# Graph attention with a conditioned self feature on one core: some loads moved in SP's queue, three setup matmul groups split into 32-output pieces

## The chip, the core and the metric

The kernel runs on one core of a Trainium2 chip. A core has a matrix engine (TensorE, PE in the profile, with PEld for its weight loads), three engines for elementwise work (VectorE, DVE; ScalarE, ACT; GpSimd, POOL), a queue engine that here issues nearly all transfers (SyncE, SP), and 16 DMA engines that carry them out. SBUF is the on-chip memory of 128 partitions, PSUM holds what TensorE writes, HBM (DRAM) is outside. The metric is device time in microseconds. All data are float32, but for the integer mask.

## The reference

For each of 16 batches there are 512 rows of 512 features (`x`), one condition vector of 512 (`q`), and an integer adjacency `adj` of 512 x 512 x 11 labels, of which only what concerns the first 20 rows is used.

```
row_zero  = x.sum(-1) == 0
self_feat = [x, where(row_zero, 0, q)] @ W_self.T + b_self
for d in 0, 1:
    A    = (adj, adj transposed)[d][:, :, :20, :]
    kv   = self_feat[:, :20]
    qh   = (self_feat @ Wq[d].T + bq[d])      in 16 heads of 32
    kh   = (kv        @ Wk[d].T + bk[d])      in 16 heads of 32
    aff  = where(A.sum(-1) > 0, qh . kh / sqrt(32), -9e15) + A @ w_bias + b_bias
    w    = softmax(aff over the 20)
    out += (w @ kv) @ Wout[d] per head + bout[d]
result = x + relu(self_feat + out)
```

## The kernel before, in words

**Setup.** Much is folded into small tables before the loop. `kv_terms` (L531) makes the 320 columns of `kv` for all batches (20 rows x 16 batches) in four PSUM banks `ps_kv`, the reduction cut in four steps k that follow the arrival of their weights. ACT turns them into `kvT`. `key_rows` (L577) multiplies `kvT` by the key weights into `ps_k` for each direction d and each of four groups of 128 features; ACT and DVE turn the result into `khD`, the keys as differences from the first one. `keys` (L660) folds the query weights into the keys: it is called in 22 bursts of 8 matmuls (the last of 4) of shape 32 x 128 into `ps_g`, which ACT (L684) and DVE (L686) scale into stages `st`; the stages go to SBUF for batch 0 and to DRAM (`g_d`, `g1_d`) for the others. Between the bursts, other setup work is put by a written list (`plan`, L714): `values` (L636, `ps_v`, the rows of `kv` times the output weights, parked in DRAM), `bias_scores`, the flags of the first batches (`ps_nz`), and the self feature of batch 0 (`self_feat`, L191, `ps_sf`).

**Forms of a matmul.** A program matmul of float32 shows as two weight loads and two matmul records. A 128-output matmul writes 128 PSUM partitions and uses the whole array; in the 32-output form the same work is four matmuls, each with 32 of the 128 weight columns, which write 32 partitions each and stand in four quarters of the array. The loop's scores and products and `ps_sf` have the 32-output form already; `ps_kv`, `ps_k` and `ps_v` have the 128-output one (`ps_v` of the last 64 rows a 64-output one).

**Loop.** 16 batches b, each in four tiles nt of 128 rows. The order on every engine is written out by hand and kept as written. A tile's step on TensorE is `scores` (L346: 64 matmuls into `ps_s`, from the self feature and the folded keys `g`). `weigh` (L364), `expo`, `normal` and `turn` make the softmax on DVE, ACT, POOL and DVE: the mask and bias tile `full` is added, the maximum taken and subtracted, the exponential taken, and after the next tile's start the sum, the division and the transpose. `full` is built by POOL (`full_add`, L336) from `cq` (the scores' biases) and `both` (the masks, spread by ACT). Each tile also carries parts for the next batch: its self feature by seven block products (`product`, L246, into `ps_a`, `ps_d`, `ps_c`; `x_sum` on POOL makes their differences; `partial` and `joined` on DVE combine them, `partial` with the row flags `nz`), its masks (`mask_mul`, `mask_count`, `mask_sum`, `mask_spread`), and its row sums (`row_sum` on ACT from `xn`, from which `row_mask` writes the flags to `nz_d`). In tile 2 TensorE makes the output of the batch before (`attend`, L417, 24 matmuls into `ps_o`: the output run); `finish` adds the self feature on DVE (four times) and takes the relu on ACT (four times), and POOL adds x (`residual`).

**Queues.** SP issues the loop's transfers in the order of the code and stops at each until what it waits for is done. `behind` (L95) puts a load behind an instruction kept in `done`. An iteration has 22 transfers there: flags `nz` (L173), biases `cq` in four (L116), masks `adj` in two halves (h = 0: "first masks", of tiles 0 and 1; h = 1: "second masks"), raw rows `xn` in two, x in two, keys `g` in two halves (L124), values `vd` in four, outputs in four, the write of `nz_d`. In the compiled program each transfer also waits until the one eight places earlier has landed.

Of the kernel before, what the change touches and what calls it, by code (L numbers as in the profile page):

```python
# [13 lines left out]
P = 128  # L14
# [4 lines left out]
def gat_kernel(  # L19
# [20 lines left out]
    nc = tc.nc  # L40
# [70 lines left out]
    def load_adj(b, h, ins=None):  # L111
        t = adjs[b, h] = load.tile([P, 2, S * L], I32, tag="adj", name=f"adj{b}_{h}", bufs=3)
        a = adj[b, h * 2 * P : (h + 1) * 2 * P].rearrange("(t p) d m l -> p t (d m l)", p=P)
        behind(nc.sync.dma_start(t, a), ins)

    def load_cq(b):  # L116
        cqs[b] = load.tile([P, HL, S], F32, tag="cq", name=f"cq{b}")
        for a in range(HL):
            nc.sync.dma_start(
                cqs[b][bass.ts(a, R)].rearrange("p h m -> p (h m)"),  # L120
                cq_d[b : b + 1, bass.ts(a, HL)].rearrange("b h d m -> b (h d m)").partition_broadcast(R),
            )
# [50 lines left out]
    def load_nz(b, ins=None):  # L173
        nzs[b] = load.tile([P, N], F32, tag="nz", name=f"nz{b}")
        behind(nc.sync.dma_start(nzs[b], nz_d[b : b + 1].partition_broadcast(P)), ins)
# [117 lines left out]

    def joined(b, n, key, f, l):

        nc.vector.tensor_add(
            block(b, f, l), parts[b, key][:, : 2 * HN].rearrange("p (i n) -> p i n", i=2), us.pop((b, n))
        )

# [132 lines left out]
    def finish(b, o, banks):  # L432

        for c in range(C):
            add = nc.vector.tensor_add(o[:, c], banks[c], sfs[b][:, c])  # L435
            if c == 0:
                done["add"] = add
        for c in range(C):
            relu = nc.scalar.activation(o[:, c], o[:, c], AF.Relu, bias=bo[:, c : c + 1])  # L439
            if c == 0:  # L440
                done["relu"] = relu

    def residual(b, c, o):
# [9 lines left out]
    with tc.tile_pool(name="setup", bufs=1) as sp, tc.tile_pool(name="ps_acc", bufs=4, space=PSUM) as acc["pool"]:  # L453
# [18 lines left out]
        with tc.tile_pool(name="setup_k", bufs=1) as sk:  # L472
# [56 lines left out]
            kv_ps = [bank(f"ps_kv{fc}") for fc in range(C)]  # L529

            def kv_terms(fc, k):  # L531
                nc.tensor.matmul(  # L532
                    kv_ps[fc][:, :BM], ws_v[:, k, bass.ts(fc, P)], xkv[:, k],
                    start=(k == 0), stop=(k == C - 1),
                )

            for k in range(2):
                for fc in range(C):
# [38 lines left out]
            def key_rows(d, jc):  # L577

                ps = bank(f"ps_k{d}{jc}")
                for k in range(C):  # L580
                    nc.tensor.matmul(  # L581
                        ps[:, :BM], wk_sb[d][:, k, bass.ts(jc, P)], kvT[:, k],
                        start=(k == 0), stop=(k == C - 1),
                    )
                p3 = ps[:, :BM].rearrange("p (b m) -> p b m", m=NG)
                kh0 = msk.tile([P, B], F32, tag="kh0", name=f"kh0{d}{jc}", bufs=4)
                nc.scalar.activation(kh0, p3[:, :, 0], AF.Identity, bias=bk_sb[:, d, jc : jc + 1])
                nc.vector.scalar_tensor_tensor(
                    khD[:, d * C + jc].rearrange("p (b m) -> p b m", m=ND), p3[:, :, 1:],
                    bk_sb[:, d, jc : jc + 1], kh0.unsqueeze(2).to_broadcast([P, B, ND]),  # L590
                    ALU.add, ALU.subtract,
                )
# [18 lines left out]
        with tc.tile_pool(name="setup_g", bufs=4) as sg:  # L611
# [24 lines left out]
            def values(t, ds, k):  # L636


                rows = min(P, BM - t * P)
                if k == 0:  # L640
                    held[1 + t // 2] = bank(f"ps_v{t}{ds[0]}")
                ps = held[1 + t // 2]
                for i, d in enumerate(ds):
                    nc.tensor.matmul(  # L644
                        ps[bass.ds(i * rows, rows)], kvT[:, k, bass.ds(t * P, rows)], wo_sb[:, d, k],
                        start=(k == 0), stop=(k == C - 1),
                    )
                if k == C - 1:
                    v = msk.tile([P, H * S], F32, tag="full", name=f"v{t}{ds[0]}")[:, :F]
                    nc.vector.tensor_copy(v, ps)  # L650
                    for i, d in enumerate(ds):
                        nc.gpsimd.dma_start(
                            vw_d[d, :, bass.ds(t * P, rows)].rearrange("c r w -> r c w"),
                            v[bass.ds(i * rows, rows)].rearrange("p (c w) -> p c w", c=C),
                        )
# [113 lines left out]
    with tc.manual_schedule():  # L769
# [11 lines left out]
        for b in range(B):  # L781
# [7 lines left out]
            for nt in range(NT):  # L789
# [64 lines left out]
                if nt == 1:  # L854
                    if b > 0:
                        joined(b, 2, "c", 0, 1)
                    if b > 0 and more:
                        load_nz(b + 1, done["exp"])
                        load_cq(b + 1)
                    normal(*prev)  # L860
                    if b > 0 and more:
                        load_adj(b + 1, 1, done["normal"])
                    if b == 0:
                        self_feat(0, 1, 1)
                    for g in range(2):
                        scores(b, nt, g, ps[g])
                    if b == 0:
                        self_copy(0, 1, 1)
                    if last:
                        for c in (0, 1):  # L870
                            nc.scalar.activation(biased[:, c], sfs[b][:, c], AF.Identity, bias=bo[:, c : c + 1])
                    s = weigh(b, nt, pair)
                    expo(s)
                    turn(*prev)
                    if more:
                        x_sum(b + 1, 2)
                        x_sum(b + 1, 3)
                    full_add(b, 2)
                    if last:
                        for c in (0, 1):  # L880
                            nc.gpsimd.tensor_add(biased[:, c], biased[:, c], xs[b][:, c])  # L881

                if nt == 2:
                    if more:
                        mask_mul(b + 1, 0)
                    else:
                        full_add(b, NT - 1)
                    if b > 0:
                        banks = [bank(f"ps_o{b - 1}_{q}", q) for q in range(4)]
                        attend(b - 1, banks)  # L890
                        o = work.tile([P, C, N], F32, tag="o", name=f"o{b - 1}")
                        finish(b - 1, o, banks)
                        if b + 2 < B:
                            load_xn(b + 2, 0, done["add"])
                            load_xn(b + 2, 1, done["relu"])
                    normal(*prev)
                    for g in range(2):
                        scores(b, nt, g, ps[g])
                    if more:
                        product(b + 1, 1)  # L900
                        product(b + 1, 2)
                    s = weigh(b, nt, pair, (lambda: partial(b + 1, 1, 0, 0)) if more else None)
                    expo(s)
                    turn(*prev)
                    if b > 0 and more:
                        load_keys(b + 1, range(2), done["exp"])
                    if more:
                        full_add(b, NT - 1)
                    if b > 0:
                        for c in (0, 1):  # L910
                            residual(b - 1, c, o)

                if nt == 3 and more:
                    mask_count(b + 1, 0)
                    product(b + 1, 6)
                    new_self(b + 1)
                    joined(b + 1, 1, "d", 0, 0)
                    x_sum(b + 1, 4)
                    if b + 2 < B:
                        for j in range(4):  # L920
                            row_sum(b + 2, j)
                    normal(*prev)
                    partial(b + 1, 2, 0, 1)
                    mask_sum(b + 1, 0)
                    if b > 0:
                        load_keys(b + 1, range(2, C), done["masks"])
                    mask_spread(b + 1, 0)
                    for g in range(2):
                        scores(b, nt, g, ps[g])
                    product(b + 1, 7)  # L930
                    product(b + 1, 5)
                    s = weigh(b, nt, pair, lambda: partial(b + 1, 3, 1, 1))
                    expo(s)
                    turn(*prev)
                    if b > 0:
                        residual(b - 1, 2, o)
                        store()
                        load_values(b)
                        residual(b - 1, 3, o)
                    full_add(b + 1, 0)  # L940
# [105 lines left out]
```

## Time and profile before

| what | us |
|---|---|
| median of 3 runs (591.52 to 592.68) | 591.74 |
| the profiled execution, whole | 593.27 |
| its span, first to last instruction | 591.5 |
| TensorE busy | 578.7 (98%) |
| VectorE busy | 492.3 (83%) |
| ScalarE, GpSimd busy | 395.6, 384.2 |
| setup, up to the first scores | 92.5 |

The span is the time from the first to the last instruction; the whole execution has 1.77 us around it. In the chain that ended last a row holds the start, the length and the work (engine, tile, line, number of records), "issue" being time in which the engine waited for nothing that the profile shows. In rows of a timeline the first two numbers are the same, and in brackets stands the idle time before. Rows of DMA issues give the count, the size and the median time from issue to landing. DVE's row of digits is its busy share in tenths in 40 equal slices of the span (14.8 us each). "q8 instruction" is the queue that brings TensorE's instructions to the core.

### The profile page before, as it was taken

To read this page: it belongs to the slowest core of one execution; us is meant where nothing else is said; L and a number is where in the kernel's file an instruction comes from. 1 tells how busy PE (TensorE), PEld (TensorE's weight loads), DVE (VectorE), ACT (ScalarE), POOL (GpSimd) and SP (SyncE) were. 2 spreads that over 40 slices of the span, in tenths; PEclk is the share of its full clock that TensorE was granted. 3 is DMA by queue.
4 is the path that set the end of the run, shared out by engine and by line. 5 is a ranking of instruction groups with operands and counts; after the bars stand their busy time and mean duration, and the time that the engine had idled before them with its cause. 6 is when DMAs were issued, how large, how long until landed. Compare 5 with 4: busy or idle time off the path is not lost.

```text
span 591.5 us, 30038 instructions
## 1 busy us (share of the span) xinstructions
PE 578.7 (98%) x13180; PEld 439.7 (74%) x13180; DVE 492.3 (83%) x785; ACT 395.6 (67%) x1162; POOL 384.2 (65%) x351
## 2 busy tenths in 40 slices
PE   8999999999999999999999999999999999999994
PEld 6654547888978687787878787788787878787882
DVE  0495565889898888999999999888989898989896
ACT  1234644587877677768686868677787877777661
POOL 2315663638677675758686777675858677776774
PEclk9999999999999999999999999999999999999997
DMA  8998999857848485767676766757585748582503
GB/s 294 385 406 299 332 376 329 257 126 199 223 154 229 155 236 148 206 168 209 184 208 163 223 173 202 171 181 208 164 217 170 216 149 232 158 238 85 167 13 142
DMA packets 98129, 124.10 MB, mean 210 GB/s; under 512 B 19952, under 2 KB 70160, under 8 KB 95952
## 3 DMA queue, kind: packets, MB, share of 16 engines
q1 hardware_dynamic: 96752, 120.31, 67.1%
q8 instruction: 103, 1.69, 1.2%
q0 software_dynamic: 672, 1.36, 1.0%
q10 hardware_dynamic: 576, 0.53, 0.3%
q14 instruction: 26, 0.21, 0.1%
HBM read 82.30 MB, written 40.24 MB: 207 GB/s over the span
## 4 chain that ended last, share of the span: by engine, by line
PE 94%; DVE 3%; DMA 1%; issue 1%; ACT 0%; POOL 0%; SPq 0%; DVEq 0%; POOLq 0%; ACTq 0%
PE ps_s L353 44%; PE ps_a L279 17%; PE ps_c L279 8%; PE ps_o L426 6%; PE ps_d L279 4%; PE ps_v L644 3%; PE ps_k L581 3%; PE ps_sf L202 2%; DMA ws_q<-in_wsT 1%; PE ps_kv L532 1%; DVE o L435 0%; PE ps_nz L186 0%; DVE wt L415 0%; DVE ps_s L371 0%; DVE sm L406 0%
## 5 line engine op out<-in xcount | busy, mean ns | idle before, releaser
L353 PEld LDWEIGHTS ps_s<-g,sf 128*32 128x32 f32 x8192 | 264.0, 110 | 19.8 <-issue 12.2
L353 PE MATMUL ps_s<-g,sf 128*32 128x152 f32 x8192 | 277.3, 293 | 0.5 <-ACT st L684 0.5
L334 ACT COPY both<-add 32x80 f32<-32x80 f32 x512 | 130.9, 256 | 54.8 <-DVE add L325 49.0
L408 POOL TENSOR_TENSOR s<-s,sm 128x640 f32<-128x640 f32 x63 | 80.3, 1275 | 98.0 <-DVE sm L407 98.0
L341 POOL TENSOR_TENSOR full<-cq,both 128x640 f32<-128x640 f32 x64 | 100.1, 1565 | 30.3 <-issue 24.3
L314 ACT ACTIVATE prod<-adj,wb_sb 128x80 f32<-128x80 int32 x330 | 112.5, 432 | 0.0
L380 ACT ACTIVATE s<-s 128x640 f32<-128x640 f32 x63 | 46.5, 738 | 69.4 <-DVE s L375 69.0
L444 POOL TENSOR_TENSOR o<-o,x 128x512 f32<-128x512 f32 x60 | 75.9, 1285 | 0.0
L367 DVE TENSOR_TENSOR full<-ps_s,full 128x608 f32<-128x608 f32 x63 | 49.1, 779 | 32.1 <-PE ps_s L353 26.6
L406 DVE TENSOR_REDUCE sm<-s 128x32 f32<-128x640 f32 x63 | 50.9, 808 | 8.8 <-ACT s L380 8.6
L279 PE MATMUL ps_a<-t,ws_s 128*32 128x246 f32 x960 | 55.5, 370 | 0.0
L371 DVE TENSOR_REDUCE ps_s<-full 128x32 f32<-128x640 f32 x63 | 52.2, 828 | 2.2
L415 DVE STREAM_TRANSPOSE wt<-s 128x640 f32<-128x640 f32 x63 | 52.8, 839 | 0.1
L375 DVE TENSOR_TENSOR s<-full,ps_s 128x640 f32<-128x640 f32 x63 | 51.6, 818 | 1.1
L426 PE MATMUL ps_o<-wt,vd 32*32 32x512 f32 (+5 forms) x816 | 40.8, 581 | 3.7 <-DVE wt L400 2.0
L279 PEld LDWEIGHTS ps_a<-t,ws_s 128*32 128x32 f32 x960 | 32.2, 110 | 15.5
L325 DVE TENSOR_REDUCE add<-prod 128x80 f32<-128x960 f32 x32 | 36.8, 1150 | 6.3 <-ACT prod L314 4.4
L244 POOL TENSOR_TENSOR t<-x 128x492 f32<-128x492 f32 x30 | 34.4, 1148 | 10.1 <-DVE full L367 5.2
L439 ACT ACTIVATE o<-o,bo 128x512 f32<-128x512 f32 x60 | 38.2, 708 | 0.6 <-POOL biased L881 0.6
L435 DVE TENSOR_TENSOR o<-ps_o,sf 128x512 f32<-128x512 f32 x60 | 36.8, 672 | 1.0 <-PE ps_o L426 1.0
L286 DVE SCALAR_TENSOR_TENSOR u<-nz,qw,ps_a 128x246 f32<-128x246 f32 x90 | 36.6, 449 | 0.0
L244 POOL TENSOR_TENSOR t<-x,t 128x492 f32<-128x492 f32 x30 | 34.4, 1147 | 1.2
(238 smaller groups left out, 722.7 us busy)
## 6 DMA issues: line engine op xcount, KB each, us to landing
g_d<-st SPq DMA_DIRECT2D x16, 1064.0 KB, 5.9
g<-g_d SPq DMA_DIRECT2D x28, 608.0 KB, 5.2
out_T<-o SPq DMA_DIRECT2D x60, 256.0 KB, 4.7
xn<-in_xn SPq DMA_DIRECT2D x28, 512.0 KB, 3.6
x<-in_xT SPq DMA_DIRECT2D x28, 512.0 KB, 4.3
adj<-in_adj SPq DMA_DIRECT2D x32, 440.0 KB, 5.0
nz<-nz_d SPq DMA_DIRECT2D x14, 256.0 KB, 4.0
wk<-in_wkT SPq DMA_DIRECT2D x2, 1024.0 KB, 8.0
```

The lines of the kernel that those rows point to most:

```text
L244: nc.gpsimd.tensor_sub(t, one, two)
L279: nc.tensor.matmul(to, lhs, x[:, k], start=start, stop=stop, skip_group_check=n != 2)
L314: nc.scalar.activation(p[:, :, l], a[:, :, l], AF.Identity, scale=wb_sb[:, l : l + 1])
L334: nc.scalar.copy(adds[b, h][bass.ts(a, R), :, g], add[r].rearrange("p (t m) -> p t m", t=2))
L341: nc.gpsimd.tensor_add(f, cqs[b].unsqueeze(1).to_broadcast(shape), adds[b, nt // 2][:, nt % 2].unsqueeze(2).to_broadcast(shape),)
L353: nc.tensor.matmul(bank[bass.ts(a, R), bass.ts(j, WD // HL)], sfs[b][:, k, bass.ds(nt * P + (2 * g + j) * R, R)], keys[:, k, a], start=(k ...
L371: nc.vector.tensor_reduce(mx, f, AX.X, ALU.max)
L375: nc.vector.tensor_sub(s, f, mx.unsqueeze(3).to_broadcast(full))
L408: done["normal"] = nc.gpsimd.tensor_mul(s, s, sm.unsqueeze(3).to_broadcast(full))
L415: nc.vector.transpose(wts[b][:, nt], s.rearrange("p a h m -> p (a h m)"))
L426: nc.tensor.matmul(banks[a][bass.ds(at // 2 * DH, n * DH)].rearrange("p (t n) -> p t n", n=32), vd[r, bass.ds(at * DH, n * DH)], wt[r, :, ...
L444: nc.gpsimd.tensor_add(o[:, c], o[:, c], xs[b][:, c])
```

## The change

Two independent parts.

In the setup, each matmul of `ps_kv`, `ps_k` and `ps_v` becomes four (two for the last 64 rows of `ps_v`) of 32 outputs. The sums, their order over k and the results are the same.

In the loop, nine transfers of an iteration move in SP's queue. The flags `nz` of the next batch go from tile 1 to tile 2, behind `finish`; they still wait for the latest exponential, which is now that of tile 1 instead of tile 0. The two loads of `xn` wait for the last of the four output additions and for the second relu, instead of the first of each. The second masks go from tile 1, where they waited for `normal`, to the end of tile 2, behind its exponential, and the biases `cq` follow them there. The first half of the keys goes from the end of tile 2 (behind its exponential) into tile 3, behind `joined`; the second half stays behind `mask_sum` in tile 3. In the after, the order in SP's queue is: flags, xn, xn, second masks, four biases, two outputs, two halves of keys, an output, four values, an output, x, x, write of the flags, first masks.

```diff
@@ -293,7 +293,7 @@
 
     def joined(b, n, key, f, l):
 
-        nc.vector.tensor_add(
+        done["joined"] = nc.vector.tensor_add(
             block(b, f, l), parts[b, key][:, : 2 * HN].rearrange("p (i n) -> p i n", i=2), us.pop((b, n))
         )
 
@@ -433,11 +433,10 @@
 
         for c in range(C):
             add = nc.vector.tensor_add(o[:, c], banks[c], sfs[b][:, c])
-            if c == 0:
-                done["add"] = add
+            done["add"] = add
         for c in range(C):
             relu = nc.scalar.activation(o[:, c], o[:, c], AF.Relu, bias=bo[:, c : c + 1])
-            if c == 0:
+            if c == 1:
                 done["relu"] = relu
 
     def residual(b, c, o):
@@ -529,10 +528,11 @@
             kv_ps = [bank(f"ps_kv{fc}") for fc in range(C)]
 
             def kv_terms(fc, k):
-                nc.tensor.matmul(
-                    kv_ps[fc][:, :BM], ws_v[:, k, bass.ts(fc, P)], xkv[:, k],
-                    start=(k == 0), stop=(k == C - 1),
-                )
+                for a in range(HL):
+                    nc.tensor.matmul(
+                        kv_ps[fc][bass.ts(a, R), :BM], ws_v[:, k, bass.ds(fc * P + a * R, R)], xkv[:, k],
+                        start=(k == 0), stop=(k == C - 1),
+                    )
 
             for k in range(2):
                 for fc in range(C):
@@ -578,10 +578,11 @@
 
                 ps = bank(f"ps_k{d}{jc}")
                 for k in range(C):
-                    nc.tensor.matmul(
-                        ps[:, :BM], wk_sb[d][:, k, bass.ts(jc, P)], kvT[:, k],
-                        start=(k == 0), stop=(k == C - 1),
-                    )
+                    for a in range(HL):
+                        nc.tensor.matmul(
+                            ps[bass.ts(a, R), :BM], wk_sb[d][:, k, bass.ds(jc * P + a * R, R)], kvT[:, k],
+                            start=(k == 0), stop=(k == C - 1),
+                        )
                 p3 = ps[:, :BM].rearrange("p (b m) -> p b m", m=NG)
                 kh0 = msk.tile([P, B], F32, tag="kh0", name=f"kh0{d}{jc}", bufs=4)
                 nc.scalar.activation(kh0, p3[:, :, 0], AF.Identity, bias=bk_sb[:, d, jc : jc + 1])
@@ -641,10 +642,11 @@
                     held[1 + t // 2] = bank(f"ps_v{t}{ds[0]}")
                 ps = held[1 + t // 2]
                 for i, d in enumerate(ds):
-                    nc.tensor.matmul(
-                        ps[bass.ds(i * rows, rows)], kvT[:, k, bass.ds(t * P, rows)], wo_sb[:, d, k],
-                        start=(k == 0), stop=(k == C - 1),
-                    )
+                    for a in range(rows // R):
+                        nc.tensor.matmul(
+                            ps[bass.ds(i * rows + a * R, R)], kvT[:, k, bass.ds(t * P + a * R, R)], wo_sb[:, d, k],
+                            start=(k == 0), stop=(k == C - 1),
+                        )
                 if k == C - 1:
                     v = msk.tile([P, H * S], F32, tag="full", name=f"v{t}{ds[0]}")[:, :F]
                     nc.vector.tensor_copy(v, ps)
@@ -854,12 +856,7 @@
                 if nt == 1:
                     if b > 0:
                         joined(b, 2, "c", 0, 1)
-                    if b > 0 and more:
-                        load_nz(b + 1, done["exp"])
-                        load_cq(b + 1)
                     normal(*prev)
-                    if b > 0 and more:
-                        load_adj(b + 1, 1, done["normal"])
                     if b == 0:
                         self_feat(0, 1, 1)
                     for g in range(2):
@@ -890,6 +887,8 @@
                         attend(b - 1, banks)
                         o = work.tile([P, C, N], F32, tag="o", name=f"o{b - 1}")
                         finish(b - 1, o, banks)
+                        if more:
+                            load_nz(b + 1, done["exp"])
                         if b + 2 < B:
                             load_xn(b + 2, 0, done["add"])
                             load_xn(b + 2, 1, done["relu"])
@@ -903,7 +902,8 @@
                     expo(s)
                     turn(*prev)
                     if b > 0 and more:
-                        load_keys(b + 1, range(2), done["exp"])
+                        load_adj(b + 1, 1, done["exp"])
+                        load_cq(b + 1)
                     if more:
                         full_add(b, NT - 1)
                     if b > 0:
@@ -915,6 +915,8 @@
                     product(b + 1, 6)
                     new_self(b + 1)
                     joined(b + 1, 1, "d", 0, 0)
+                    if b > 0:
+                        load_keys(b + 1, range(2), done["joined"])
                     x_sum(b + 1, 4)
                     if b + 2 < B:
                         for j in range(4):
```

## The prediction

> **What bounds the kernel now.** I read the page's shares first, then the chain that ended last, then SP's queue in one iteration.
>
> ```profile
> DVE  0495565889898888999999999888989898989896
> ...
> q8 instruction: 103, 1.69, 1.2%
> ...
> PE 94%; DVE 3%; DMA 1%; issue 1%; ACT 0%; POOL 0%; SPq 0%; DVEq 0%; POOLq 0%; ACTq 0%
> ```
>
> TensorE makes 94% of the chain: time is won only where PE's work shortens or where PE stands. The chain through the setup, and one piece of batch 0:
>
> ```profile
> 11.45 2.39 PE ps_kv L532 x8
> ...
> 17.43 8.94 PE ps_k L581 x32
> ...
> 27.34 2.35 PE ps_k L581 x8
> ...
> 37.86 2.36 PE ps_k L581 x8
> ...
> 41.69 1.91 PE ps_v L644 x4
> ...
> 51.54 1.01 PE ps_v L644 x4
> ...
> 59.41 1.73 PE ps_sf L202 x32
> ...
> 83.97 1.87 PE ps_v L644 x8
> ...
> 110.66 0.77 issue
> ```
>
> ps_sf is already in the 32-output form: 16 matmuls of 256 columns, four sets of four, 1.73 us, or 0.43 us a set, which is 1.69 ns a column (a program matmul is two records, one for each half of the f32 work). The 128-output form in the same place, between two bursts of keys, takes 1.91 for two matmuls of 512 columns, the same 1024 columns.
>
> In the loop the chain is PE without a break but for one place, the output run (attend, L426, 48 records):
>
> ```profile
> 164.12 2.60 PE ps_o L426 x47
> ...
> 195.02 1.04 PE ps_o L426 x25
> 196.45 2.10 PE ps_o L426 x23
> ...
> 226.92 0.98 PE ps_o L426 x4
> ...
> 258.97 2.17 PE ps_o L426 x48
> ...
> 289.44 2.17 PE ps_o L426 x48
> ...
> 381.08 1.05 PE ps_o L426 x27
> ...
> 413.08 2.84 PE ps_o L426 x48
> ...
> 444.22 2.17 PE ps_o L426 x48
> ```
>
> From one uncut run to the next is 30.47 us (258.97 to 289.44). The iteration that begins at 164.12 takes 30.90, at 195.02 31.90, at 226.92 32.05, at 381.08 32.00, at 413.08 31.14: 0.43 + 1.43 + 1.58 + 1.53 + 0.67 = 5.6 us lost in five of fifteen runs. The cut moves: record 25, then 4, then not in the run, later 27. An iteration is 784 records (four tiles of 128, seven products of 32, 48), each a weight load and a matmul, and by the compiled program 10 waits: 1,578 instructions, 42 over a multiple of 256, so a mark every 256 instructions comes 21 records earlier each time. 25 to 4 is that step, and 1.69 MB in 103 transfers is 16.4 KB each. PE stands at the edge of a block of instructions that has not arrived.
>
> **The change, part by part.** *Setup matmuls in 32-output form.* 16 matmuls of ps_kv, 32 of ps_k, 16 of ps_v with 128 outputs and 8 with 64 become 272 of 32 outputs. Priced at 1.69 ns a column, four sets of 320 take 2.16 us and two of 512 1.73.
> - Values: eight stretches of 1.91, so 8 x 0.18 = 1.44; the 64-row ones 2 x 0.14 (1.01 to 0.87) and 0.14 (1.87 to 1.73). Gross 1.9. About 0.4 returns as waiting: in the middle of the setup two bursts of keys wait for DVE copies that stand behind the mask's reductions, which hang on POOL. Net 1.5.
> - Key rows: four stretches of 2.35, 4 x 0.19 = 0.76, and 0.29 in the first one (8.94 against 8.65). DVE's third slice (29.6 to 44.4 us) is at 9 tenths, so its copies set the pace for part of this, and the first stretch waits for ACT's kvT. I take 0.4.
> - ps_kv: 0.23 at 11.45; the later stretch (0.09) is not what kvT waits for. 0.2.
>
> Together -2.1; ends -3.2 (all of it) and 0 (every saving becomes a wait or a drain, below).
>
> *A rule against it.* The Trainium skill (TensorEngine Tiling (Array Packing), Key Properties) says that a change of the array's tiling mode drains TensorE. The after still changes shape at every burst, so by that rule alone this part is worth nothing and the sum would be +0.7 instead of -1.4. The trace shows no such drain on entering ps_sf behind a burst of another shape: 1.69 ns a column is the rate of the loop's scores too (4.00 us for 124 records of 152 columns, last row below: 1.70). What the 128-output form loses, it loses at its entry.
>
> *800 more PE instructions.* 200 more matmuls at four instructions each; 800 = 3 x 256 + 32, so every block edge of the loop falls 16 records earlier. In batch 0 PE stands 0.77 us (110.66) at an edge among the products, whose records of 246 columns last 52 ns by the rate above: it needs the block 16 x 52 = 0.8 us sooner. It asks for it one block earlier, among scores (32 ns a record), 0.5 sooner: +0.3; ends -0.8 (the stall goes) and +0.8 (the block comes no sooner).
>
> *The loop's loads.* SP's queue in the iteration whose output run is at 319.92:
>
> ```profile
> 314.45 0.37 SPq L114 DMA_DIRECT2D adj<-in_adj  x1
> 317.69 0.34 SPq L175 DMA_DIRECT2D nz<-nz_d  x1
> 318.08 2.95 SPq L119 DMA_DIRECT2D cq<-cq_d  x4
> 321.14 0.39 SPq L114 DMA_DIRECT2D adj<-in_adj  x1
> 323.93 4.10 SPq L109 DMA_DIRECT2D xn<-in_xn  x2
> 330.65 0.38 SPq L130 DMA_DIRECT2D g<-g_d  x1
> 331.12 1.50 SPq L449 DMA_DIRECT2D out_T<-o  x2
> 334.95 0.38 SPq L130 DMA_DIRECT2D g<-g_d  x1
> ```
>
> Flags, biases and second masks (317.69 to 321.5) leave the stretch before the output run. Would that free the instruction block? It is asked for about one block earlier: some 102 records of scores of 32 ns, 3.3 us before the run begins (for the cut at record 25). The flags are issued 2.2 us before the run, after the request; what is in flight at the request are the first masks, issued 5.5 us before the run and landing in 5.0 (median, below). They stay. So I count no gain there; ends -5.6 (all stalls go) and +4. By the 21-record step the edges of before lie at records 46, 25 and 4, then at 48, 27 and 6, then at 50 of the run; 16 earlier they cut it at 30, 9, 32, 11 and 34, and in two iterations fall 10 records ahead of it. Behind record 32 the run's second matmul shape begins, before which PE finishes the first anyway; an edge there costs like the one at 46 (0.4): 1.5 + 1.5 + 0.4 + 1.5 + 0.4 = 5.3 against 5.6: 0, rounded.
>
> ```profile
> g<-g_d SPq DMA_DIRECT2D x28, 608.0 KB, 5.2
> nz<-nz_d SPq DMA_DIRECT2D x14, 256.0 KB, 4.0
> adj<-in_adj SPq DMA_DIRECT2D x32, 440.0 KB, 5.0
> g<-g_d SPq DMA_DIRECT2D x1, 1216.0 KB, 8.0
> ...
> 322.67 0.74 ACT L380 ACTIVATE s<-s 128x640 f32<-128x640 f32 x1 [2.85 <-DVE s L375]
> 329.88 0.74 ACT L380 ACTIVATE s<-s 128x640 f32<-128x640 f32 x1 [0.38 <-DVE s L375]
> 328.22 0.84 DVE L286 SCALAR_TENSOR_TENSOR u<-nz,qw,ps_a 128x246 f32<-128x246 f32 x2
> 331.42 0.66 DVE L296 TENSOR_TENSOR sf<-ps_d,u 128x492 f32<-128x492 f32 x1
> 340.68 4.00 PE ps_s L353 x124
> ```
>
> - Flags: now behind exp of tile 1, 323.45, landing about 327.5; first used at 328.2 by the partial product, for which product 6 waits on PE some 0.6 us later still. 0, hidden under the tile's addition and maximum on DVE; with that cover gone each us late is a us of PE.
> - Raw rows (xn): behind the last output add and the second relu, some 2 and 0.6 us later. ACT's row sums take them as they land. 0.
> - Second masks behind exp of tile 2 (330.65), then biases: used in the next tile 0 by ACT and POOL some 9 us on. 0.
> - Keys: the first half waits for joined (over at 332.08), but stands behind masks, four bias loads (1.9 to 2.95 us of SP's time) and two outputs: issued 333.9 to 335.0 where it was 330.65. Landing in 5.2: 339.1 to 340.2; scores need it at 340.68. The second half, at 334.95 to 335.4, now has the first right ahead: between 5.2 and 8.0 (both halves in one transfer), so 340.2 to 343.4; it is needed 2.07 later than the first, 342.75. Margin at the middle 0.5 to 1 us. I take 0.2 in all fourteen iterations; ends 0 and 14 x 0.7 = 10.
> - x behind it (SP waits for the eighth transfer back) may slip by 1 us; POOL's first difference takes it and has idle time after. 0.
>
> A further +0.2 for blocks that come late in the crowded keys' stretch. Sum: -2.1 + 0.3 + 0 + 0.2 + 0.2 = -1.4. The profiled execution took 593.27 (span 591.5 and 1.77 around it), 1.53 over the median 591.74. 593.27 - 1.4 = 591.87, which in medians is 590.3.
>
> **Rivals.** Each with the -1.4 of the sum, in medians.
> 1. *Keys late (slower).* One mechanism: the two halves share the 10 us before scores with masks, biases and outputs. From a second-half latency of 7.4 us (342.75 - 335.4) on, PE waits each iteration; at 0.4 us, 14 x 0.4 = 5.6, less 1.4: 595.9. For: 8.0 for the double transfer. Against: that one ran behind other setup traffic.
> 2. *The output run's stalls go (the loads were in the way).* -1.4 - 5.3: 585.0. For: they are the nearest transfers to the run. Against: the order of request and issue above. By the Trainium skill (DMA: Bandwidth & Descriptors, Queues, rings and completion order) a DMA engine takes turns between queues packet by packet, which also lets only the transfer under way delay a block; no view here shows the turns.
> 3. *Setup gives nothing* (drain, or evictions set the pace): -1.4 + 2.1: 592.4, no change.
> 4. *More runs cut:* where the edge lies 10 records before the run, the block also waits behind the first masks: two runs x (1.5 + 10 records of 32 ns) = +3.6, less 1.4: 593.9. Against: that request falls before the first masks are issued, or just at it.
>
> **How the numbers follow.** Forecast 0.50 (own range 589.2 to 591.6), rival 1 0.22, rival 2 0.08, rival 3 0.12, rival 4 0.08. 0.2%, about what a measurement of this kernel tells from no change, is 1.2 us: 590.55 to 592.9. The forecast lies two thirds below that band (0.34), with rival 2 faster 0.42; same: 0.16 of the forecast and 0.08 of rival 3, 0.24; slower 0.34. The range 588.5 to 596 leaves out rival 2 and the upper part of rival 1.
>
> **What would show it.** Setup: ps_v stretches of 1.73 and ps_k of 2.16 in the chain, the first scores at about 90.4 instead of 92.5. Output runs cut near records 30, 9 and 11, about 5.3 us in all: step right; all at 2.17: rival 2. No wait of ps_s for g: keys step right; an idle PE before scores of tile 0 naming g: rival 1. An uncut setup with waits for st or khD in the place of the savings: rival 3. Wrong altogether if the loop's 30.47 us changes in uncut iterations.

## The result, and the profile after

| what | before | after |
|---|---|---|
| median, us (11 runs each, side by side) | 591.4 (588.89 to 592.68) | 596.03 (592.55 to 597.66) |
| ratio after to before | | 1.0078, 95% interval 1.0058 to 1.0099 |
| profiled execution, whole / span | 593.27 / 591.5 | 595.52 / 593.7 |
| TensorE busy | 578.7 | 577.1 |

The change makes the kernel 0.8% slower (4.6 us), where 590.3 and "a little faster" was forecast. The profiled execution of before lies 1.9 us above its median, that of after 0.5 below, so the two traces show 2.2 us of the difference.

From the page of after: the engines' busy time, the queue of instructions, the chain's shares, the scores' group (busy, mean, idle before and its releaser), and the keys' loads.

```profile
PE 577.1 (97%) x13580; PEld 430.2 (72%) x13580; DVE 491.8 (83%) x785; ACT 395.9 (67%) x1162; POOL 385.3 (65%) x351
...
q8 instruction: 107, 1.75, 1.2%
...
PE 82%; DVE 9%; DMA 3%; issue 2%; ACT 1%; POOL 1%; SPq 1%; DVEq 0%; POOLq 0%; ACTq 0%
...
L353 PE MATMUL ps_s<-g,sf 128*32 128x152 f32 x8192 | 279.1, 293 | 4.6 <-DMA g<-g_d 1.6
...
g<-g_d SPq DMA_DIRECT2D x28, 608.0 KB, 5.8
```

TensorE works 1.6 us less than before and the kernel ends later: its share of the chain falls from 94% to 82%, while DVE's grows from 3% to 9%, the DMA's from 1% to 3%, and SP's queue from 0 to 1%. The scores' idle time grows from 0.5 to 4.6 us and has a name that the page of before does not have, the keys `g`; the row of before is

```profile
L353 PE MATMUL ps_s<-g,sf 128*32 128x152 f32 x8192 | 277.3, 293 | 0.5 <-ACT st L684 0.5
```

The keys' loads take 5.8 us instead of 5.2 (medians).

The chain of after through setup, batch 0 and part of the loop:

```profile
16.18 8.84 PE ps_k L582 x128
25.99 2.29 PE ps_k L582 x32
...
39.65 1.85 PE ps_v L646 x16
...
90.05 4.34 PE ps_s L353 x128
...
102.75 0.43 issue
...
107.99 1.93 issue
...
132.93 2.17 PE ps_o L426 x48
...
163.40 1.07 PE ps_o L426 x30
165.00 2.08 PE ps_o L426 x18
...
226.19 2.17 PE ps_o L426 x48
...
241.14 5.66 DMA g<-g_d
...
258.30 2.17 PE ps_o L426 x48
288.78 2.17 PE ps_o L426 x48
```

and the same places in the chain of before:

```profile
92.52 4.34 PE ps_s L353 x128
...
133.59 2.17 PE ps_o L426 x48
```

The spans differ by four stretches. The first key rows begin at 16.18 instead of 17.43 (-1.25; how much of this is the change's comes below). From there to the first scores it takes 73.87 instead of 75.09 (-1.22). From the first scores to the first output run it takes 42.88 instead of 41.07 (+1.81), with more "issue" at 102.75 and 107.99. From the first output run to the end of the span it takes 460.8 instead of 457.9 (+2.86). An iteration without a stand (a stand is time in which TensorE is idle) is unchanged: 30.48 from 258.30 to 288.78.

The last stretch is the keys. This is the chain of after across the end of tile 2 and the next scores of tile 0:

```profile
360.20 0.74 ACT s L380
...
361.10 0.25 SPq L114
...
361.40 0.58 SPq L119
...
362.03 1.48 SPq L119
...
365.00 0.38 SPq L448
...
365.47 6.07 DMA g<-g_d
371.53 0.14 issue
371.67 4.34 PE ps_s L353 x128
```

Tile 2's exponential lets the second masks go (L114), then four bias loads (L119) hold SP for 3 us (the row below, from the timeline of SP), then two outputs (L448); only at 365.47, 4.5 us behind the end of the exponential, the first half of the keys is issued, and it lands as TensorE already waits. The second half is issued 0.5 us behind it and lands after 7.5 us.

```profile
361.40 3.04 SPq L119 DMA_DIRECT2D cq<-cq_d  x4
```

The starts of the weight loads show the stands one by one: in nine of the loop's fourteen iterations two neighbouring starts at the scores of tile 0 lie 0.3 to 1.3 us apart (usual there is 0.1 to 0.2). Five of the nine wait for the first half, four for the second. The list of TensorE's waits (total in us, times, longest) names only some of them:

```profile
PE ps_s L353 <- DMA g<-g_d: 1.6, 3, 0.9
PE ps_s L353 <- issue: 1.3, 3, 0.7
...
PE ps_s L353 <- DVE sf L296: 0.9, 1, 0.9
```

The 0.9 us put down to DVE is at 497.85, where the second half of the keys landed at 497.74: a wait for several things carries the name of one of them. The nine intervals between output runs that hold such a wait are 6.6 us over 30.47 together; 2.0 of this is at stands that have nothing to do with keys, so by subtraction about 4.6 us are the keys'.

### The profile page after: what moved, and what is told of

Same layout as the page of the kernel before. It is cut to its first block, busy times and chain, and to the rows that moved or that the text cites. A ratio compares the mean times of both kernels' runs of the same rounds, so it can differ in the third digit from the quotient of the medians.

```text
span 593.7 us, 30828 instructions
## 1 busy us (share of the span) xinstructions
PE 577.1 (97%) x13580; PEld 430.2 (72%) x13580; DVE 491.8 (83%) x785; ACT 395.9 (67%) x1162; POOL 385.3 (65%) x351
## 4 chain that ended last, share of the span: by engine, by line
PE 82%; DVE 9%; DMA 3%; issue 2%; ACT 1%; POOL 1%; SPq 1%; DVEq 0%; POOLq 0%; ACTq 0%
PE ps_s L353 39%; PE ps_a L279 13%; PE ps_c L279 7%; PE ps_o L426 4%; PE ps_d L279 3%; PE ps_v L646 3%; PE ps_k L582 3%; DMA g<-g_d 3%; PE ps_sf L202 2%; DVE o L435 2%; PE ps_kv L532 2%; DVE sm L406 1%; DVE wt L415 1%; DVE full L367 1%; DVE ps_s L371 1%
## 5 line engine op out<-in xcount | busy, mean ns | idle before, releaser
L426 PE MATMUL ps_o<-wt,vd 32*32 32x512 f32 (+5 forms) x816 | 37.7, 579 | 2.8 <-DVE wt L400 2.0
L166 ACT ACTIVATE xn<-xn 128x512 f32<-128x512 f32 x56 | 34.6, 619 | 4.1 <-DMA xn<-in_xn 4.0
```

Of the source, the lines that this page charges most:

```text
L426: nc.tensor.matmul(banks[a][bass.ds(at // 2 * DH, n * DH)].rearrange("p (t n) -> p t n", n=32), vd[r, bass.ds(at * DH, n * DH)], wt[r, :, ...
```

## The experiments

Each ratio is against the kernel before on the same chip, which ran at 591.17 for the first four, 590.96 for the next four and 593.11 for the last four (another chip), so ratios and not medians are compared between groups. The ratio is an estimate with its 95% interval and not the quotient of the two medians (in e2_loads the medians alone give 1.0060, the estimate 1.0078). The first theory (K) was that the late keys cost the time; its rival (P) that the shifted edges of TensorE's instruction blocks (256 instructions each) do, wherever the loads stand.

**e1_setup: the setup's part alone.** The kernel before with the three loops over 32-output pieces; the queue as before.

> The kernel before with the 32-output matmuls of the setup alone; SP's queue as before. Theory K (the later keys cost the time, with a longer stand at an instruction block in batch 0): first scores 2.4 us earlier, 1.2 to 1.8 us of it given back in batch 0, the loop loses about the 6 us of before with its cut output runs at records near 30, 9 and 11, no score waits for keys: 0.5 to 1.5 us below before. Rival P (the 16-record shift of the block edges costs the time, wherever the loads stand): 2 to 4.5 us above before, with new stands at block edges in the loop.

Measured: 591.14 against 591.17, ratio 1.0003 (0.9987 to 1.0019). The chain:

```profile
17.43 8.84 PE ps_k L583 x128
...
91.31 4.34 PE ps_s L353 x128
...
108.63 2.21 issue
```

The first key rows begin at 17.43, exactly as in the profile of before, although `ps_kv` ahead of them has the new form. In all runs with the old setup and seven warm-up matmuls that row starts between 16.48 and 17.91, in those with the new one between 15.97 and 18.10: it is not the change that sets it, and the -1.25 above is no gain. From key rows to scores 73.88 (after: 73.87), and 2.21 us of "issue" in batch 0. The setup alone is neither faster nor slower than can be told: P's 2 us are outside the interval, and so is all but the near end of what K expected.

**e2_loads: the moved loads alone.**

The change with its three setup loops taken back, here the first:

```diff
-                for a in range(HL):
-                    nc.tensor.matmul(
-                        kv_ps[fc][bass.ts(a, R), :BM], ws_v[:, k, bass.ds(fc * P + a * R, R)], xkv[:, k],
...
+                nc.tensor.matmul(
+                    kv_ps[fc][:, :BM], ws_v[:, k, bass.ts(fc, P)], xkv[:, k],
...
```

> The kernel before with the loop's moved loads alone; setup and block edges as before. Theory K: scores of tile 0 wait for keys in most iterations, 5 to 9 us together, of which up to 5 come back where output runs are no longer cut: 1 to 5 us above before. Rival P: within 1 us of before, and the cut runs (25, 4, 27, 6) stay or go without a new wait.

Measured: 594.72 against 591.17, ratio 1.0078 (1.0041 to 1.0115), the ratio of the whole change. The loads are the loss; the block edges here are those of before, so P falls. In its trace (the slowest of its seven executions, 601.93) eight of the fourteen iterations have the stand at the scores of tile 0, five for the first half of the keys and three for the second.

**e3_keys_first: after, with the keys ahead again.**

```diff
                     if b > 0 and more:
+                        load_keys(b + 1, range(2), done["exp"])
                         load_adj(b + 1, 1, done["exp"])
                         load_cq(b + 1)
...
-                    if b > 0:
-                        load_keys(b + 1, range(2), done["joined"])
```

> The changed kernel, but the first half of the keys is issued at the end of tile 2, behind the exponential and ahead of the second masks and biases. Theory K: no score waits for keys; from after's median 596.0 the waits of 5 to 7 us go: 589 to 591, 0.5 to 2.5 us below before. Rival P: the key waits go but the stands at block edges move or grow in their place: 594 or more.

Measured: 591.16 against 591.17, ratio 1.0003 (0.9983 to 1.0023). The whole loss is gone with one load moved: it stands ahead of masks, biases and two outputs again, and waits for the exponential instead of `joined`. One stand, of 0.7 us by the weight loads, is left ahead of the scores' second half in fourteen iterations.

**e4_phase: the block edges alone.**

```diff
-            for _ in range(7):
+            for _ in range(15):
                 nc.tensor.matmul(warm[:, :P], ones, ones, start=True, stop=True)
```

> The kernel before with 15 warm-up matmuls instead of 7: 32 more PE instructions ahead of everything, in time in which PE waits for the first weights, so every block edge falls 16 records earlier, as in after; nothing else differs. Theory K: batch 0 loses 0.3 to 1.5 us more at its edges, the loop about as before: 0 to 1.5 us above before. Rival P: 2 to 4.5 us above.

Measured: 592.41 against 591.17, ratio 1.0020 (1.0007 to 1.0032). That is 1.2 us, inside K's 0 to 1.5 and below P's 2 to 4.5, and far from the 4.6 of after. Not all of it need be the edges': the first key rows begin at 18.71 here, later than in any run with seven warm-up matmuls (18.10 at most). The stand in batch 0 is at the place that after has it, and only some tenths longer than the 0.77 of before:

```profile
110.62 1.12 issue
```

With the keys as cause, the question became what makes them late: the later place behind `joined` (KW), or the masks and biases that are now ahead of them in SP's queue (KQ).

**e5_keys_later: the first half of the keys behind joined, nothing else moved.**

```diff
-                        load_keys(b + 1, range(2), done["exp"])
...
                     joined(b + 1, 1, "d", 0, 0)
+                    if b > 0:
+                        load_keys(b + 1, range(2), done["joined"])
```

> The kernel before with one move: the first half of the keys goes from the end of tile 2 into tile 3, behind joined; masks, biases, flags and raw rows stay where they were. Theory KW (the later point itself is too late: joined and the two outputs ahead): scores wait for keys in half the iterations or more, 2 to 4 us above before. Theory KQ (it is the masks and bias loads ahead of the keys in SP's queue that make them late): within 1 us of before, no score waiting for keys.

Measured: 590.19 against 590.96, ratio 0.9987 (0.9974 to 1.0000). No score waits for keys. The later place behind `joined`, with two outputs ahead, costs nothing by itself: KW falls. The view of the keys' loads (landing times: least, median, most):

```profile
DMA to landing us min/median/max: 4.1/5.4/6.4
```

**e6_keys_behind_masks: the loads of e2_loads, but the keys wait only for the exponential and go ahead of the outputs, directly behind masks and biases.**

```diff
                         load_adj(b + 1, 1, done["exp"])
                         load_cq(b + 1)
+                        load_keys(b + 1, range(2), done["exp"])
...
-                    if b > 0:
-                        load_keys(b + 1, range(2), done["joined"])
```

> The kernel before with the moved loads of after, but the first half of the keys stays in tile 2 and waits for the exponential, directly behind the second masks and the four bias loads (no wait for joined, outputs behind it). Setup and block edges as before. KQ: 2 to 4 us above before, with waits for keys as in e2_loads. KW: within 1 us of before, no waits for keys.

Measured: 597.07 against 590.96, ratio 1.0099 (1.0070 to 1.0127). The loss is there without the wait for `joined`: KQ. The profiled execution is the fastest of its six (593.64, the others 596.77 to 599.58), so it shows only a part of the loss. Its chain, its list of TensorE's waits and its keys' landing times, in this order:

```profile
364.08 7.83 DMA g<-g_d
371.91 0.14 issue
372.05 2.27 PE ps_s L353 x64
```

```profile
PE ps_s L353 <- DMA g<-g_d: 4.3, 5, 1.4
```

```profile
DMA to landing us min/median/max: 4.3/6.0/8.2
```

Here the second half, behind the outputs, is the late one: 7.83 us from issue to landing, and the second 64 records of the scores of tile 0 wait for it.

**e7_setup_same_edges: the setup's part with the block edges of before.** The last 64 rows of `values` keep the 64-output form, so that 768 instructions, three whole blocks, are added.

```diff
-                    for a in range(rows // R):
+                    w = R if rows == P else rows
+                    for a in range(rows // w):
...
```

> The kernel before with the 32-output matmuls of the setup, but the last 64 rows of the values keep the 64-output form: 768 more PE instructions, three whole blocks, so the block edges of the loop lie as in before. If the setup's saving reaches the end (2.1 less 0.3 for the rows left out) and the shifted edges took it in e1_setup: 589.0 to 589.8, 1.4 to 2.2 us below before, the stand in batch 0 at 0.8 us. If batch 0 takes it back wherever the edges lie (the block comes at a time that does not depend on when PE starts the scores): 590.6 to 591.4, the stand in batch 0 at 2 us or more.

Measured: 590.27 against 590.96, ratio 0.9997 (0.9979 to 1.0015). Between the two expectations: the stand in batch 0 is back at the size of before (row below), and still no gain can be measured.

```profile
108.47 0.84 issue
```

**e8_keys_first_same_edges: e3_keys_first with the same trick.**

> The kernel e3_keys_first (all of after, the first half of the keys ahead of masks and biases) with the block edges of before, by the 64-output form of the last 64 rows. If the shifted edges cost 1.2 us: 589.5 to 590.3 (591.16 less 1.2, plus 0.3). If the shift costs nothing beside the earlier start: 591 to 591.6.

Measured: 591.53 against 590.96, ratio 1.0001 (0.9983 to 1.0018). No gain from the edges here either: 591.53 lies where a shift that costs nothing was expected.

Next, which of the loads ahead of the keys does it: the masks' 440 KB (M) or SP's time for four bias loads (B).

**e9_biases_back and e10_masks_back: e2_loads with the biases, or the second masks, put back into tile 1.**

```diff
e9:                     if b > 0 and more:
+                        load_cq(b + 1)
                     normal(*prev)
...
-                        load_cq(b + 1)
e10:                    normal(*prev)
+                    if b > 0 and more:
+                        load_adj(b + 1, 1, done["normal"])
...
-                        load_adj(b + 1, 1, done["exp"])
```

> e2_loads (594.72, 3.5 us above before) with the four bias loads put back into tile 1; the second masks stay ahead of the keys. Theory M (the masks' 440 KB, whose transfer fills the DMA engines, delay the keys): still 2.5 to 4 us above before, with waits for keys. Theory B (the four bias loads, 2 to 3 us of SP's time, delay the keys): within 1 us of before, no waits for keys. If each has its part: 1.2 to 2.5 us above.

> e2_loads with the second masks put back into tile 1, behind normal; the four bias loads stay ahead of the keys. Theory M: within 1 us of before. Theory B: still 2.5 to 4 us above. If each has its part: 1.2 to 2.5 us above.

Measured against 593.11: e9 594.85, ratio 1.0038 (1.0010 to 1.0065); e10 592.86, ratio 0.9984 (0.9966 to 1.0002). Biases alone ahead of the keys cost nothing that can be told; masks alone cost something, by the estimate about half of what both cost together (1.0078 in e2_loads, on another chip). So the masks have a part of their own. That the biases add to it behind the masks is not shown by the times, whose intervals overlap, but the traces show how they would. On average over the fourteen iterations SP issues the first half of the keys 10.4 us behind the end of the output run in e5_keys_later, e10_masks_back and e12_both_back, 10.6 in e9_biases_back, but 12.6 in e2_loads and in after: either group alone leaves it where `joined` puts it, both together hold SP 2 us longer, so that both halves are mostly issued 0.5 us apart instead of 2.2. The masks alone lengthen the way from issue to landing, to 6.2 us for either half (5.4 and 5.5 in e10_masks_back). The profiled execution of e9 (593.57, while its runs go from 592.74 to 599.17) shows no score waiting for keys, though both halves take longer:

```profile
DMA to landing us min/median/max: 5.2/6.2/7.0
```

What its longer executions lose by was not seen.

**e11_keys_later_setup: e5_keys_later with the setup of e7_setup_same_edges.**

> The two parts that cost nothing, together: e5_keys_later (590.19 against 590.96) with the setup of e7_setup_same_edges (590.27). If their gains add: 589 to 589.8, 1.2 to 2 us below before. If batch 0 takes the earlier start back, as in e7_setup_same_edges, and the keys' move is worth nothing: 590.2 to 591.

Measured: 592.79 against 593.11, ratio 0.9991 (0.9975 to 1.0008): no gain to be measured. No kernel of this study is faster than before by the 0.2% that can be told.

**e12_both_back: after, with only the second masks and the biases back in tile 1.**

> The changed kernel with only the second masks and the biases put back into tile 1: setup in 32-output form, flags and raw rows later, keys behind joined. Theory KQ (masks and biases ahead of the keys are what after loses by): 590 to 592, no score of tile 0 waiting for keys. If the later flags, raw rows or keys cost by themselves: 593 or more.

Measured: 592.71 against 593.11, ratio 0.9989 (0.9968 to 1.0010). All other edits of the change (32-output setup, later flags, later raw rows, later keys) together cost nothing that can be told. Its output runs in the chain:

```profile
164.31 1.07 PE ps_o L426 x30
165.50 2.08 PE ps_o L426 x18
195.89 0.99 PE ps_o L426 x9
196.94 2.16 PE ps_o L426 x39
...
349.56 1.07 PE ps_o L426 x32
351.13 1.12 PE ps_o L426 x16
380.92 2.83 PE ps_o L426 x48
```

## Why the prediction was wrong, step by step

**Keys: the step that failed.** The prediction put the first half at 333.9 to 335.0 and the second right behind it, gave the second a latency "between 5.2 and 8.0", and, with a margin of 0.5 to 1 us at the middle, priced the waits of all fourteen iterations together at 0.2 us. They cost about 4.6, and that term is what failed. Order and moment were right: in after the two are issued 0.5 us apart, behind masks, biases and outputs. The size was not. The second half takes 7.5 us at 365.97 and 6.8 on average over the fourteen (7.0 or more in the nine where it is issued 0.5 us behind the first), near the upper end, which was the row of a transfer of the same two halves together (8.0); the first half was late too, five times. On average both halves do land in time, 17.9 and 20.3 us behind the end of the output run, where an iteration of before without a stand needs them at 18.4 and 20.4. But that leaves 0.5 and 0.2 us, less than was said, and the latencies of single loads run from 4.2 to 7.5. Rival 1 had the mechanism and nearly the price: its threshold was 7.4 us of latency, its cost 5.6 us, and its time 595.9 against 596.03 measured. That the times agree so well is in part luck: it had a wait for the second half in each iteration where nine of fourteen wait, five of them for the first, and it counted 1.4 us of gain that no run shows. The argument against it, that the 8.0 was measured behind other setup traffic, had no weight: here masks, biases and outputs stood ahead.

**Setup: direction right, size too large, and worth nothing at the end.** Expected were stretches of 1.73 for `ps_v` and 2.16 for `ps_k`; the chain of after has 1.85 and 2.29. The error is in the reading of `ps_sf`. Two rows of TensorE's timeline of before (start, length, partitions x columns, records) show its forms:

```profile
59.35 1.80 PE L202 MATMUL ps_sf<-x,ws_v 128*32 128x236 f32 x32
...
86.75 1.93 PE L202 MATMUL ps_sf<-x,ws_v 128*32 128x256 f32 x32
```

The stretch of 1.73 that I priced by has 236 columns, not 256: the first 20 rows come from elsewhere. That is 1.83 ns a column, and that 1.69 met the 1.70 of the scores was chance. With 256 columns the chain of before has

```profile
86.82 1.86 PE ps_sf L202 x32
```

which is what `ps_v` takes for 1024 columns in the 32-output form (1.85). From 1.85 for 1024 columns and 2.29 for 1280 a column is 1.72 ns and the entry of a stretch 0.09 us; from 1.91 and 2.35 in the 128-output form the column is the same 1.72 and the entry 0.15. So the 32-output form saves 0.06 us a stretch, whatever its length, not 0.18. From the first key rows to the first scores the old setup took 74.6 to 75.2 us in six profiles, the new one 73.9 to 74.2 in four: 0.8 us on average in place of 1.9 for values and key rows. That the first scores of after begin at 90.05, close to the 90.4 that was forecast, is luck: 1.25 us of it is the earlier start of the key rows. In no run did that reach the end as a gain that can be told from none (e1_setup, e7_setup_same_edges, e11_keys_later_setup). Rival 3 was right about what the setup is worth at the end. The rule that the prediction set against this part, that a change of tiling mode drains TensorE (the Trainium skill, TensorEngine Tiling (Array Packing), Key Properties), was put aside too early: the "no drain" was argued from the miscounted columns. No run here separates a drain from other costs of entering a stretch.

**800 more instructions: the place right, the size too small.** +0.3 was taken for batch 0. The shift alone (e4_phase) makes the stand 1.12 instead of 0.77, as worked out, and the shorter setup alone (e7_setup_same_edges) 0.84; both together make 1.93 in after, 2.21 in e1_setup and 1.66 in e3_keys_first and e12_both_back, 0.9 to 1.4 us more than before instead of 0.3. Why the two together cost more than their sum stays open.

**Output runs.** The edges came where the step of 21 and the shift of 16 put them: records 30, 9 and 32 in e12_both_back, 30 in after. That the moved loads change nothing there was wrong or at least not shown: of the predicted 5.3 us after lost some 1.8 (the run at 163.40 takes 3.68 instead of 2.17, the one at 381.80 takes 2.46). Part of rival 2 came true, then. How much of this the loads did can't be said: runs with the loads of before also differ from each other (in e5_keys_later four runs are cut and lose about 3.2, in before five lose 5.6). In their place after has stands of 0.5 to 1.0 at other edges in the loop, 2.0 us together by the spacing of the weight loads.

**The rest.** Flags, raw rows, x, the biases and the masks' own use at 0: right (e3_keys_first has all of these moves and loses nothing). An uncut iteration stays at 30.48: right. The sum in the trace of after: 1.2 won in the setup and 1.25 by weights that came earlier, 1.8 lost in batch 0, 2.9 lost in the loop, where the keys' 4.6 and new stands of 2.0 outweigh what the output runs lost less. From the -1.4 of the forecast to the +4.6 measured in medians it is 6.0: the larger part is what the keys cost above their 0.2, and most of the rest the 2.1 of the setup, which never arrived at the end.

## What to carry to other kernels

Price a load that is moved behind others in an issuing queue by the slowest row of the same data that the profile has, together with everything now ahead of it, and compare that with the moment of use: a margin of half a microsecond is no margin where the latencies spread over three (4.2 to 7.5 us here), and it was lost in nine of fourteen iterations. In this kernel the later issue point alone cost nothing; what stood between the point and the load did. Put what is needed last behind what is needed first. And before a rate is read from a stretch, read the shape of its instructions: the view by form keeps 236 and 256 columns apart, the chain shows both under one name.

## What the runs showed of the hardware

- Two loads of 608 KB took 5.3 and 6.8 us on average behind masks, biases and outputs (after), with the second at 7.0 to 7.5 where it was issued half a microsecond behind the first. That closeness is not needed for it: in e6_keys_behind_masks, 2.2 us apart, they took 5.3 and 7.0. With masks and biases out of their way, also 2.2 us apart, they took 5.2 and 5.3 (e12_both_back).
- The edges of TensorE's instruction blocks move with the instructions added ahead of them: 8 more warm-up matmuls, 32 instructions, moved the stand of batch 0 from the records of `ps_d` to those of `ps_a`. The whole kernel took 0.2% longer (1.0007 to 1.0032), of which the later start of the key rows may be a part.
- The spread of a kernel's executions does not tell of late keys: 592.55 to 597.66 in after and 589.43 to 591.48 in e5_keys_later, but also 588.61 to 594.53 in e3_keys_first, and 590.30 to 597.52 in the last group's 35 executions of before.
